# Attention and scan kernel on one core: empty places that do preparation work, an end of its own for the last block, and program order on every engine

## The chip, the cores and the metric

The kernel runs on one core of one Trainium2 chip. A core has five engines that run at the same time and meet through semaphores: TensorE (PE in the profile; its weight loads are PEld), VectorE (DVE), ScalarE (ACT), GpSimd (POOL) and SyncE (SP), which issues the transfers here. The metric is the device time of one execution in microseconds. Before the change it is 3108.49 us, the median of three runs (3106.8 to 3109.73).

## The reference

Four images of 128 channels by 4096 positions go through two layers, all in float32. Cut to what matters:

```python
# layer 0, per image: x is (128, 4096) after a group norm
v, gate = split(sigmoid(conv_bn(x, Wvg)))
q, k    = conv_bn(x, Wq) * SCALE, conv_bn(x, Wk)        # 64 channels each
out     = softmax(q.T @ k) @ v.T * gate                 # 4096 x 4096 scores
x       = x0 + conv_bn(out, Wp)

# layer 1, per image: t is (4096, 128), h = layernorm(t)
q       = h @ W
t       = t + softmax(q @ q.T) @ h                      # symmetric scores
Wx      = layernorm(t) @ Wffn.T
# over all four images:
Wx      = batchnorm(Wx)                                 # mean and variance over 16384 rows
y_t     = sigmoid(Wx_t + y_(t-1) @ V.T)                 # a scan over 4096 steps
x       = t + y
```

## The kernel before

For each image the kernel runs `layer0` and `layer1`; the scan follows behind all four. It works in blocks of 512 queries (`NB` = 8 per image). In `layer0` a block is 16 pairs of key tiles. In `layer1` the scores are symmetric: a block of scores `(n, a)` with `a < n` is used once as it stands (`direct`) and once transposed (`reversed_products`), so its exponentials `e` are transposed by VectorE into `dd`, turned further by 16 transfers into `tt`, and multiplied four steps later.

What is left to do for a finished block, and what prepares the next image, is cut into small functions. They wait in two queues, `pending` and `ahead`, and the main loops take one function from a queue in each step, so that its instructions come between the large products:

```python
        ahead: deque = deque()
        pending: deque = deque()

        def nothing():
            pass
        ...
        def flush(until=None):
            while pending and until not in done:
                pending.popleft()()

        def attention(score_mm, bias, scale, weigh, finish, need):
            ...
            for n in range(NB):
                acc = first = None
                for p in range(PAIRS):
                    need(n, p)
                    ps = ps_s.tile([P, 2, QB], F32, tag="s", name="ps")
                    for h in range(2):                              # scores of a pair
                        lhsT, rhs = score_mm(n, p, h)
                        nc.tensor.matmul(ps[:, h, :], lhsT=lhsT, rhs=rhs, start=True, stop=True)
                    e = ep.tile([P, 2, QB], F32, tag="e", name="e")
                    nc.scalar.activation(e, ps, AF.Exp, scale=scale)
                    ...                                             # acc += e on VectorE
                    fifo.append((n, p, e, acc))
                    if len(fifo) > LAG:                             # LAG = 2
                        pop()                                       # value products of pair p - 2
                        ...
                    if ahead:
                        ahead.popleft()()
                    elif pending and (p % 2 == 0 or len(pending) > 6):
                        pending.popleft()()
```

`layer0` puts `[sums, nothing, denominators, projection, nothing, tokens]` in `pending` for each finished block; `nothing` leaves time for a transfer. `sums` and `projection` each end in `move`, which turns a tile through memory: one transfer out and four in.

The layer norm over the 128 channels of each row, used by both layers:

```python
        def layernorm(src, dst):
            ...
            for j in range(NQ):                       # NQ = 4
                nc.vector.bn_stats(s6, src[j])
                nc.vector.bn_aggr(mv[:, j, :], s6)
            inv_sqrt(rstd, mv[:, :, 1], EPS_LN)       # two instructions on GpSimd
            for j in range(NQ):
                nc.vector.tensor_scalar(dst[j], src[j], mv[:, j, 0:1], rstd[:, j : j + 1],
                                        ALU.subtract, ALU.mult)
```

The preparation of an image: `stats`, `mean`, `variance`, `normalise`, then `queries_keys` and `values` for chunks of 512 positions, then `gate`. For image 0 the first chunk is done ahead of everything, and `need` makes sure that the rest is ready in time; for the others the functions go into `ahead` and are taken during `layer1` of the image before.

```python
            def queries_keys(ch):
                m = bank(False)
                nc.tensor.matmul(m, lhsT=wt["qk"], rhs=xg[:, cs], start=True, stop=True)
                nc.vector.tensor_scalar(q[lo, cs], m[lo, :], ...)
                nc.scalar.activation(q[hi, cs], m[lo, :], AF.Identity, ...)
                nc.vector.tensor_scalar(k[...], m[hi, :], ...)

            def values(ch):
                m = bank(True)
                for i in range(4):
                    nc.tensor.matmul(m[:, bass.ts(i, P)], lhsT=xg[...], rhs=wt["vs"], ...)
                nc.vector.tensor_tensor(vc, m, bc, ALU.add)
                nc.scalar.activation(vc, vc, AF.Tanh, scale=0.5)
                nc.vector.tensor_scalar(vc, vc, 0.5, 0.5, ALU.mult, ALU.add)
        ...
        def need(n, p):
            if n == 0:
                while p // 4 > 0 and n_ahead - len(ahead) < 6 * (p // 4):
                    ahead.popleft()()
```

A step of `layer1`, and what a finished block leaves to do there:

```python
                    for i in range(2):
                        ...                                        # 2 score products, 2 exponentials,
                        ...                                        # 2 transposes into dd if turned
                        fifo.append((n, a, i, e, o))
                        clock += 1
                        if len(fifo) > LAG:
                            direct()
                        if turned and turned[0][0] <= clock:
                            reversed_products()                    # 4 products with tt, VectorE sums
                        if pending:
                            pending.popleft()()
                        elif ahead:
                            ahead.popleft()()
                    if turns(n, a):
                        ...                                        # 16 transfers tt <- dd
                        turned.append((clock + 4, n, a, t))

            def finish(n):
                ...
                nc.sync.dma_start(t, t_d[b, n])
                def tokens():     # mt: 4 transposes of oacc; t1 = mt * rinv + t; h2 = layernorm(t1)
                def result():     # mr: 4 transposes of t1; ScalarE copies; store to t2_d
                def turn():       # mh: 4 transposes of h2; ScalarE copies to th
                def inputs():     # mw: product of wt["f"] and th; bn_stats; copy to wx or wxs
                if b == B - 1 and n == 0:
                    pending.extend([tokens, turn, inputs, result])
                else:
                    pending.extend([tokens, result, turn, inputs])
```

All four take their PSUM bank from `ps_m`, which has one buffer; `h2`, `th`, `t1` and `t2` have one buffer each in the pool `work`.

Behind the last block come a range test over all denominators (`ok`), the pools of the scan, and the scan:

```python
        ok = big.tile([P, 2, 2 * B * NT], F32, tag="oacc", name="ok")
        ...                                                        # two compares, one reduction
    with ExitStack() as st:
        scan = st.enter_context(tc.tile_pool(name="scan", bufs=1))
        ...
        mv = scan.tile([P, 2], F32, name="bn_mv")
        nc.vector.bn_aggr(mv, bn_st.rearrange("p a b -> p (a b)"))
        gain = scan.tile([P, 1], F32, name="gain")
        inv_sqrt(gain, mv[:, 1:2], EPS_BN)
        ...
        for k, i in enumerate(steps):                              # 44 steps of 2 halves
            ...                                                    # product with V, sigmoid on ScalarE,
                                                                   # VectorE: preload, t2 += y
```

The order in which an engine's instructions stand in the built program is not the order in which the code emits them: a scheduler chooses it at compile time, by priority and by its own estimate of times.

Of the kernel before, what the change touches and what calls it, by code (L numbers as in the profile page):

```python
# [18 lines left out]
P = 128  # L19
B, C, N = 4, 128, 4096  # L20
DQ = 64
# [28 lines left out]
def conv_attn_hybrid_kernel(  # L50
# [78 lines left out]
    def inv_sqrt(dst, var, eps):  # L129
# [5 lines left out]
    fast(  # L135
        tc, x, out, t_d, t2_d, wxs_d, turn_d,
        dict(qk=w[:, DQ : DQ + P], vs=w_vs, g=w_g, ps=w_ps, a=w_a, f=w_f, vt=v_t),
        col, par, par2, bpc, bc, ident, gavg, quart, own, shift, inv_sqrt, par_ok,
    )
# [18 lines left out]
def fast(  # L158
# [7 lines left out]
    den_all = keep.tile([P, 2 * B * NT], F32, name="den_all")  # L166

    with ExitStack() as st:
# [14 lines left out]
        def nothing():  # L183
            pass
# [8 lines left out]
        def attention(score_mm, bias, scale, weigh, finish, need):  # L193
# [3 lines left out]
            o = None  # L197

# [9 lines left out]
# [5 lines that stand above are left out]
                    for h in range(2):  # L213
# [4 lines that stand above are left out]
                    if p == 0:  # L218
                        first = e
                    elif p == 1:  # L220
                        acc = accp.tile([P, 2, QB], F32, tag="acc", name="acc", bufs=2)
                        nc.vector.tensor_tensor(acc, first, e, ALU.add)
                    else:
                        nc.vector.tensor_tensor(acc, acc, e, ALU.add)  # L224
                    fifo.append((n, p, e, acc))
                    if len(fifo) > LAG:
                        pop()
                        if p == 0:
                            pop()
                    if ahead:  # L230
                        ahead.popleft()()
                    elif pending and (p % 2 == 0 or len(pending) > 6):
                        pending.popleft()()
# [232 lines left out]
        def layer1(b, h, qt):  # L466
# [74 lines left out]
            def finish(n):  # L541
# [3 lines left out]
                h2 = work.tile([P, NQ, C], F32, tag="h2", name="h2")  # L545
                th = work.tile([P, QB], F32, tag="th", name="th")
                t1 = work.tile([P, NQ, C], F32, tag="og", name="t1b")
                nc.sync.dma_start(t, t_d[b, n])

                def tokens():  # L550
# [4 lines left out]
                    m = ps_m.tile([P, NQ, P], F32, tag="m", name="mt")  # L555
# [10 lines left out]
                def result():  # L566
                    m = ps_m.tile([P, QB], F32, tag="m", name="mr")
                    for j in range(NQ):
                        nc.tensor.transpose(m[:, bass.ts(j, P)], t1[:, j, :], ident)
                    t2 = work.tile([P, QB], F32, tag="xb", name="t2")  # L570
                    nc.scalar.copy(t2, m)
                    nc.sync.dma_start(t2_d[b, :, cs], t2)

                def turn():
                    m = ps_m.tile([P, QB], F32, tag="m", name="mh")
# [4 lines left out]
                def inputs():  # L580
                    m = ps_m.tile([P, QB], F32, tag="m", name="mw")
# [10 lines left out]
                if b == B - 1 and n == 0:  # L592
                    pending.extend([tokens, turn, inputs, result])
                else:
                    pending.extend([tokens, result, turn, inputs])
# [106 lines left out]

        ok = big.tile([P, 2, 2 * B * NT], F32, tag="oacc", name="ok")
# [5 lines left out]
    with ExitStack() as st:  # L709
# [19 lines left out]
        mv = scan.tile([P, 2], F32, name="bn_mv")  # L729
        nc.vector.bn_aggr(mv, bn_st.rearrange("p a b -> p (a b)"))  # L730
        gain = scan.tile([P, 1], F32, name="gain")
# [3 lines left out]
        bias = scan.tile([P, 1], F32, name="bias")  # L735
# [458 lines left out]
```

## Time and profile before

| | |
|---|---|
| time, median of 3 | 3108.49 us |
| span of the profiled run | 3106.2 us |
| granted TensorE clock | 0.993 |
| first TensorE product | 16.25 us |
| first product of the scan | 3020.77 us |
| last store issued, end | 3082.6 us, 3106.2 us |

A line of the group lists reads: line of the code, engine, operation, tile written and tiles read, sizes, count; then busy time and mean length of one; then how long the engine stood idle just before these instructions, and what ended that idle time. A line of the list of waits reads: who waited, for whom, us in total, times, longest. A line of the timeline reads: start, length, engine, line, operation, tiles, count, and in brackets the idle time before it with what ended it. A line of the list by stretch reads: from, to, length, then busy time and count for each engine (PE, PEld, DVE, ACT, POOL), the granted clock, and the transfers' share and rate. One product in the code with 512 columns is two records here; a record on all 128 rows has 0.429 us to the next, one on half of the rows (L215, L394, two halves side by side) 0.214 us on average.

### The profile page before, as it was taken

To read this page: it belongs to the slowest core of one execution; us is meant where nothing else is said; L and a number is where in the kernel's file an instruction comes from. 1 tells how busy PE (TensorE), PEld (TensorE's weight loads), DVE (VectorE), ACT (ScalarE), POOL (GpSimd) and SP (SyncE) were. 2 spreads that over 40 slices of the span, in tenths; PEclk is the share of its full clock that TensorE was granted. 3 is DMA by queue.
4 is the path that set the end of the run, shared out by engine and by line. 5 is a ranking of instruction groups with operands and counts; after the bars stand their busy time and mean duration, and the time that the engine had idled before them with its cause. 6 is when DMAs were issued, how large, how long until landed. Compare 5 with 4: busy or idle time off the path is not lost.

```text
span 3106.2 us, 32252 instructions
## 1 busy us (share of the span) xinstructions
PE 3018.6 (97%) x10706; PEld 1362.3 (44%) x10706; DVE 1877.7 (60%) x3160; ACT 1144.8 (37%) x2018; POOL 144.5 (5%) x183
## 2 busy tenths in 40 slices
PE   7999999999999999999999999999999999999976
PEld 3444444444444444444444444444444444444432
DVE  6666656555666665655566666555566666455546
ACT  3444433333344443333334443333334444323324
POOL 0000000000000000000000000000000000000000
PEclk9999999999999999999999999999999999999988
DMA  1011143333111123334211114333321113443423
GB/s 51 28 55 55 55 111 88 91 89 92 46 55 55 55 78 93 90 89 97 73 52 55 50 43 116 88 91 93 91 56 55 49 44 121 114 104 88 98 98 157
DMA packets 233168, 241.14 MB, mean 78 GB/s; under 512 B 88480, under 2 KB 144288, under 8 KB 231968
## 3 DMA queue, kind: packets, MB, share of 16 engines
q1 hardware_dynamic: 231984, 238.18, 28.2%
q8 instruction: 88, 1.44, 0.2%
q10 hardware_dynamic: 1008, 0.79, 0.1%
q14 instruction: 88, 0.72, 0.1%
HBM read 65.80 MB, written 56.62 MB: 39 GB/s over the span
## 4 chain that ended last, share of the span: by engine, by line
PE 91%; DVE 4%; SPq 1%; POOL 1%; DMA 1%; issue 1%; ACT 0%; ACTq 0%; DVEq 0%; POOLq 0%
PE o L394 28%; PE ps L215 15%; PE ps L613 15%; PE o L501 14%; PE ot L514 12%; SPq L650 1%; PE m L243 1%; PE mw L582 1%; PE mq L487 1%; PE mp L326 1%; PE ps_r L764 1%; PE mh L577 1%; POOL rstd L132 1%; DVE t1b L559 1%; PE mp L361 1%; PE mp L346 1%
## 5 line engine op out<-in xcount | busy, mean ns | idle before, releaser
L394 PE MATMUL o<-e,nxt 64*128 64x512 f32 x4096 | 963.8, 589 | 0.0
L217 ACT ACTIVATE e<-ps 128x1024 f32<-128x1024 f32 x512 | 521.4, 1025 | 674.7 <-PE ps L215 657.5
L224 DVE TENSOR_TENSOR acc<-acc,e 128x1024 f32<-128x1024 f32 x448 | 547.6, 1222 | 236.4 <-ACT e L217 220.5
L619 ACT ACTIVATE e<-ps,shift 128x512 f32<-128x512 f32 x580 | 393.9, 684 | 749.8 <-PE ps L613 497.1
L394 PEld LDWEIGHTS o<-e,nxt 64*128 64x128 f32 x4096 | 399.0, 187 | 482.3 <-issue 474.5
L613 PE MATMUL ps<-qt 128*128 128x512 f32 x1160 | 547.8, 595 | 2.7 <-ACT qt L488 2.7
L501 PE MATMUL o<-e,h 128*128 128x512 f32 x1160 | 537.7, 592 | 0.0
L215 PE MATMUL ps<-nxt 64*128 64x512 f32 x2048 | 534.5, 596 | 1.2 <-DVE nxt L338 0.9
L514 PE MATMUL ot<-tt,h 128*128 128x512 f32 x888 | 399.8, 593 | 0.0
L624 DVE STREAM_TRANSPOSE dd<-e 128x512 f32<-128x512 f32 x444 | 286.5, 686 | 83.4 <-ACT e L619 73.1
L501 PEld LDWEIGHTS o<-e,h 128*128 128x128 f32 x1160 | 218.3, 191 | 260.7 <-issue 259.5
L613 PEld LDWEIGHTS ps<-qt 128*128 128x128 f32 x1160 | 213.4, 191 | 249.0 <-issue 224.2
L215 PEld LDWEIGHTS ps<-nxt 64*128 64x128 f32 x2048 | 194.5, 187 | 231.5 <-issue 158.8
L514 PEld LDWEIGHTS ot<-tt,h 128*128 128x128 f32 x888 | 167.9, 190 | 210.0 <-issue 205.7
L519 DVE TENSOR_REDUCE slots<-tt 128x4 f32<-128x2048 f32 x111 | 250.7, 2258 | 9.7 <-DMA tt<-dd 9.4
L528 DVE TENSOR_TENSOR oacc<-oacc,ot 128x512 f32<-128x512 f32 x87 | 59.3, 682 | 209.8 <-PE ot L514 209.8
L131 POOL TENSOR_SCALAR rstd<-mv 128x4 f32<-128x4 f32 x64 | 14.6, 228 | 2456.5 <-DVE mv L268 2456.5
L619 ACT ACTIVATION_READ_ACCUMULATOR e<-ps,shift 128x1 f32 x580 | 113.9, 196 | 0.0
L448 DVE SCALAR_TENSOR_TENSOR t<-yt,rinv,t 128x128 f32<-128x128 f32 x128 | 36.6, 347 | 71.5 <-DMA yt<-turn_d 71.4
L411 POOL TENSOR_SCALAR xb<-xb,bpc 128x512 f32<-128x512 f32 x32 | 57.4, 1793 | 318.0 <-DMA xb<-in_x_dram 289.3
L132 POOL TENSOR_TENSOR rstd<-rstd,mhalf 128x4 f32<-128x4 f32 x64 | 66.4, 1038 | 5.3
L271 DVE TENSOR_SCALAR h<-t,mv,rstd 128x128 f32<-128x128 f32 x128 | 35.7, 343 | 47.1 <-POOL rstd L132 47.1
(134 smaller groups left out, 1491.7 us busy)
## 6 DMA issues: line engine op xcount, KB each, us to landing
tt<-dd SPq DMA_DIRECT2D x1776, 64.0 KB, 2.0
turn_d<-d SPq DMA_DIRECT2D x96, 256.0 KB, 2.0
t_d<-t SPq DMA_DIRECT2D x64, 256.0 KB, 2.0
nxt<-in_x_dram SPq DMA_DIRECT2D x16, 512.0 KB, 5.5
xb<-in_x_dram SPq DMA_DIRECT2D x32, 256.0 KB, 2.9
t<-turn_d SPq DMA_DIRECT2D x128, 64.0 KB, 2.0
yt<-turn_d SPq DMA_DIRECT2D x128, 64.0 KB, 2.0
qt<-turn_d SPq DMA_DIRECT2D x128, 64.0 KB, 2.0
```

Source lines behind the costliest of these rows:

```text
L132: nc.gpsimd.tensor_tensor(dst, dst, mhalf[:, :n], ALU.pow)
L215: nc.tensor.matmul(ps[:, h, :], lhsT=lhsT, rhs=rhs, start=True, stop=True)
L217: nc.scalar.activation(e, ps, AF.Exp, scale=scale)
L224: nc.vector.tensor_tensor(acc, acc, e, ALU.add)
L394: nc.tensor.matmul(o[r], lhsT=v[rs, p + h * PAIRS, :], rhs=e[rs, h, :], start=(p == 0 and h == 0), stop=(p == PAIRS - 1 and h == 1),)
L501: nc.tensor.matmul(o, lhsT=h[:, NQ * a + 2 * i + half, :], rhs=e[:, half, :], start=(a == order(n)[0] and i == 0 and half == 0), stop=(a = ...
L514: nc.tensor.matmul(ot, lhsT=h[:, NQ * n + j, :], rhs=t[:, :, j, :, :].rearrange("q p k j -> q k p j"), start=(j == 0), stop=(j == NQ - 1),)
L519: nc.vector.tensor_reduce(slots[:, bass.ts(n, NQ), a], t.rearrange("q p b k j -> q b p (k j)"), AX.XY, ALU.add,)
L528: nc.vector.tensor_tensor(oacc[:, n, :], oacc[:, n, :], o, ALU.add)
L613: nc.tensor.matmul(ps[:, half, :], lhsT=qt[:, bass.ts(at, P)], rhs=qt[:, bass.ts(n, QB)], start=True, stop=True,)
L619: nc.scalar.activation(e[:, half, :], ps[:, half, :], AF.Exp, bias=shift, accum_out=slots[:, at, n : n + 1],)
L624: nc.vector.transpose(d.rearrange("q f b k j -> q k b f j")[:, 2 * i + half], e[:, half, :].rearrange("q (b f j) -> q b f j", b=NQ, f=NQ),)
```

## The change

It has four parts:

- *Empty places.* `nothing` now takes a function from `ahead`, if there is one, and two such places stand between `result` and `turn` in `layer1`. In `attention`, functions that were in `pending` at the start are taken in every step.
- *An end of its own.* The last block of the last image puts `tokens` at the head of the queue, brings `result` ahead of `turn`, takes its tiles from the pool of `e` and its PSUM banks from the scores' pool.
- *Ahead of the scan.* The BatchNorm's small tiles lie in the pool `keep` instead of the scan's own, and one sigmoid on a single column is issued before the range test, so that the table of that function is loaded there.
- *Program order.* The whole of `fast` stands under `tc.manual_schedule()`: each engine, SyncE included, gets its instructions in the order in which the code emits them.

It is meant to keep TensorE from waiting for the layer norm, to shorten the chain between the last attention product and the scan, and to make the order of work that of the loop.

```diff
--- before.py
+++ after.py
@@ -132,11 +132,12 @@
         nc.gpsimd.tensor_tensor(dst, dst, mhalf[:, :n], ALU.pow)
 
     par_ok = const.tile([P, 4], F32, name="par_ok")
-    fast(
-        tc, x, out, t_d, t2_d, wxs_d, turn_d,
-        dict(qk=w[:, DQ : DQ + P], vs=w_vs, g=w_g, ps=w_ps, a=w_a, f=w_f, vt=v_t),
-        col, par, par2, bpc, bc, ident, gavg, quart, own, shift, inv_sqrt, par_ok,
-    )
+    with tc.manual_schedule():
+        fast(
+            tc, x, out, t_d, t2_d, wxs_d, turn_d,
+            dict(qk=w[:, DQ : DQ + P], vs=w_vs, g=w_g, ps=w_ps, a=w_a, f=w_f, vt=v_t),
+            col, par, par2, bpc, bc, ident, gavg, quart, own, shift, inv_sqrt, par_ok,
+        )
 
 
 
@@ -164,6 +165,10 @@
     keep = keep_ctx.enter_context(tc.tile_pool(name="keep", bufs=1))
     bn_st = keep.tile([P, B * NB, 6], F32, name="bn_st")
     den_all = keep.tile([P, 2 * B * NT], F32, name="den_all")
+    mv = keep.tile([P, 2], F32, name="bn_mv")
+    gain = keep.tile([P, 1], F32, name="gain")
+    bias = keep.tile([P, 1], F32, name="bias")
+    first_y = keep.tile([P, 1], F32, name="first_y")
 
     with ExitStack() as st:
         big = st.enter_context(tc.tile_pool(name="big", bufs=1))
@@ -181,7 +186,10 @@
         pending: deque = deque()
 
         def nothing():
-            pass
+
+
+            if ahead:
+                ahead.popleft()()
 
         done = set()
 
@@ -195,6 +203,7 @@
 
             fifo: deque = deque()
             o = None
+            left = len(pending)
 
             def pop():
                 nonlocal o
@@ -229,7 +238,8 @@
                             pop()
                     if ahead:
                         ahead.popleft()()
-                    elif pending and (p % 2 == 0 or len(pending) > 6):
+                    elif pending and (p % 2 == 0 or left > 0 or len(pending) > 6):
+                        left -= 1
                         pending.popleft()()
             while fifo:
                 pop()
@@ -542,9 +552,22 @@
                 cs = bass.ts(n, QB)
                 rinv = stat.tile([P, NQ], F32, tag="rinv", name="rinv")
                 t = work.tile([P, 4, NQ, 32], F32, tag="t", name="t1", bufs=2)
-                h2 = work.tile([P, NQ, C], F32, tag="h2", name="h2")
-                th = work.tile([P, QB], F32, tag="th", name="th")
-                t1 = work.tile([P, NQ, C], F32, tag="og", name="t1b")
+                if b == B - 1 and n == 0:
+
+                    one, two = (ep.tile([P, 2, QB], F32, tag="e", name="last") for _ in range(2))
+                    h2, t1 = (one[:, r, :].rearrange("q (j c) -> q j c", j=NQ) for r in range(2))
+                    th, t2 = two[:, 0, :], two[:, 1, :]
+
+                    def bank():
+                        return ps_s.tile([P, 2, QB], F32, tag="s", name="ml")[:, 0, :]
+                else:
+                    h2 = work.tile([P, NQ, C], F32, tag="h2", name="h2")
+                    th = work.tile([P, QB], F32, tag="th", name="th")
+                    t1 = work.tile([P, NQ, C], F32, tag="og", name="t1b")
+                    t2 = None
+
+                    def bank():
+                        return ps_m.tile([P, QB], F32, tag="m", name="m1")
                 nc.sync.dma_start(t, t_d[b, n])
 
                 def tokens():
@@ -552,7 +575,7 @@
                     den = den_all[:, at : at + NQ]
                     nc.vector.tensor_reduce(den, slots[:, bass.ts(n, NQ), :], AX.X, ALU.add)
                     nc.vector.reciprocal(rinv, den)
-                    m = ps_m.tile([P, NQ, P], F32, tag="m", name="mt")
+                    m = bank().rearrange("q (j c) -> q j c", j=NQ)
                     for j in range(NQ):
                         nc.tensor.transpose(m[:, j, :], oacc[:, n, bass.ts(j, P)], ident)
                     for j in range(NQ):
@@ -564,21 +587,23 @@
                     layernorm(quarters(t1), quarters(h2))
 
                 def result():
-                    m = ps_m.tile([P, QB], F32, tag="m", name="mr")
+                    nonlocal t2
+                    m = bank()
                     for j in range(NQ):
                         nc.tensor.transpose(m[:, bass.ts(j, P)], t1[:, j, :], ident)
-                    t2 = work.tile([P, QB], F32, tag="xb", name="t2")
+                    if t2 is None:
+                        t2 = work.tile([P, QB], F32, tag="xb", name="t2")
                     nc.scalar.copy(t2, m)
                     nc.sync.dma_start(t2_d[b, :, cs], t2)
 
                 def turn():
-                    m = ps_m.tile([P, QB], F32, tag="m", name="mh")
+                    m = bank()
                     for j in range(NQ):
                         nc.tensor.transpose(m[:, bass.ts(j, P)], h2[:, j, :], ident)
                     nc.scalar.copy(th, m)
 
                 def inputs():
-                    m = ps_m.tile([P, QB], F32, tag="m", name="mw")
+                    m = bank()
                     nc.tensor.matmul(m, lhsT=wt["f"], rhs=th, start=True, stop=True)
                     nc.vector.bn_stats(bn_st[:, b * NB + n, :], m)
                     m = m.rearrange("p (g i s) -> p i g s", i=L // 2, s=2)
@@ -590,9 +615,12 @@
                         nc.sync.dma_start(wxs_d[b, :, :, bass.ts(n, GB), :], wx)
 
                 if b == B - 1 and n == 0:
-                    pending.extend([tokens, turn, inputs, result])
+                    pending.appendleft(tokens)
+                    pending.extend([result, turn, inputs])
+                elif b == B - 1 and n < 4:
+                    pending.extend([tokens, result, turn, inputs])
                 else:
-                    pending.extend([tokens, result, turn, inputs])
+                    pending.extend([tokens, result, nothing, nothing, turn, inputs])
 
 
             for n in [NB - 2, NB - 1] + list(range(NB - 3, -1, -1)):
@@ -700,6 +728,8 @@
                 ahead.popleft()()
         flush()
 
+
+        nc.scalar.activation(first_y, shift, AF.Sigmoid)
         ok = big.tile([P, 2, 2 * B * NT], F32, tag="oacc", name="ok")
         nc.vector.tensor_scalar(ok[:, 0, :], den_all, DEN_LO, None, ALU.is_ge)
         nc.vector.tensor_scalar(ok[:, 1, :], den_all, DEN_HI, None, ALU.is_le)
@@ -726,13 +756,10 @@
                     banks[s][i][:, : HB * G], lhsT=ident, rhs=wxs[:, 0, :HB, :, 0],
                     start=True, stop=True, skip_group_check=True,
                 )
-        mv = scan.tile([P, 2], F32, name="bn_mv")
         nc.vector.bn_aggr(mv, bn_st.rearrange("p a b -> p (a b)"))
-        gain = scan.tile([P, 1], F32, name="gain")
         inv_sqrt(gain, mv[:, 1:2], EPS_BN)
         nc.vector.tensor_mul(gain, gain, col(GAMMA))
 
-        bias = scan.tile([P, 1], F32, name="bias")
         nc.vector.tensor_mul(bias, mv[:, 0:1], gain)
         nc.vector.tensor_sub(bias, col(BETA), bias)
```

## The prediction, written before the result was known

> **What bounds the kernel now.** I read the page's busy line and chain first, then busy time by stretch, then TensorE's waits, then the timeline of the places where TensorE stands still.
>
> ```profile
> PE 3018.6 (97%) x10706; PEld 1362.3 (44%) x10706; DVE 1877.7 (60%) x3160; ACT 1144.8 (37%) x2018; POOL 144.5 (5%) x183
> ...
> PE 91%; DVE 4%; SPq 1%; POOL 1%; DMA 1%; issue 1%; ACT 0%; ACTq 0%; DVEq 0%; POOLq 0%
> ```
>
> TensorE carries 91% of the chain that ended last; nothing else comes near. The change adds and removes no matrix product, so only TensorE's standing time, and the stretches in which TensorE is not the limit, can move. Busy time by stretch (start, warm-up, the eight attention stages, their end, the scan, the last store) says how much that is:
>
> ```profile
> 0.00:16.25 16.25, 0.00 (x0) 0.03 (x1) 7.28 (x17) 1.28 (x1) 3.68 (x13) 1.00 0.61 194
> ...
> 100.00:2950.00 2850.00, 2829.21 (x10062) 1273.80 (x10059) 1727.71 (x2852) 1047.07 (x1846) 131.97 (x156) 1.00 0.29 76
> 2950.00:3020.77 70.77, 53.95 (x155) 25.67 (x153) 33.12 (x100) 17.58 (x43) 5.98 (x11) 0.90 0.19 61
> 3020.77:3081.30 60.53, 55.19 (x172) 27.10 (x172) 53.60 (x113) 42.12 (x87) 0.00 (x0) 0.97 0.30 129
> ```
>
> The second column of numbers is TensorE's busy time. In 2850 us of attention it stands only 20.8 us; in the 71 us of their end 16.8 us; before its first product 16.25 us. The scan runs on VectorE (53.6 of 60.5), and nothing in the change touches its work. TensorE's waits name the standing time:
>
> ```profile
> PE mh L577 <- DVE h L271: 15.7, 21, 4.4
> PE ps_r L764 <- ACT y L761: 7.8, 1, 7.8
> ...
> PE mp L346 <- DVE nxt L351: 2.4, 3, 0.8
> PE mp L326 <- DVE nxt L351: 2.4, 3, 0.8
> ```
>
> The first is the one that repeats: `turn` transposes the layer norm's result `h2` and stands until VectorE has written it. Why it is not written is seen in one such place:
>
> ```profile
> 585.60 1.12 DVE L559 SCALAR_TENSOR_TENSOR t1b<-mt,rinv,t 128x128 f32<-128x128 f32 x4
> ...
> 588.77 1.04 POOL L132 TENSOR_TENSOR rstd<-rstd,mhalf 128x4 f32<-128x4 f32 x1
> 589.84 1.11 DVE L271 TENSOR_SCALAR h<-t1b,mv,rstd 128x128 f32<-128x128 f32 x4 [1.47 <-POOL rstd L132]
> ...
> 590.33 0.49 PE L577 MATMUL mh<-ident,h 128*128 128x128 f32 x2 [0.65 <-DVE h L271]
> ```
>
> The norm takes 5.4 us from 585.60 to 590.95, and the scheduler has put the transposes 4.7 us behind its start. (The products `mt` that feed it ran at 567.98, nearly 18 us sooner.) The end shows a chain of single steps:
>
> ```profile
> 3006.50 1.15 PE L577 MATMUL mh<-ident,h 128*128 128x128 f32 x4 [4.39 <-DVE h L271]
> ...
> 3015.81 1.02 DVE L730 BATCH_NORM_AGGREGATE bn_mv<-bn_st 128x2 f32<-128x192 f32 x1 [4.03 <-DMA t_d<-t]
> ...
> 3018.81 1.28 ACT L761 ACT_TABLE_LOAD   x1 [5.24 <-DVE bias L737]
> ...
> 3020.77 1.65 PE L764 MATMUL ps_r<-y,w 128*128 128x256 f32 x3 [7.82 <-ACT y L761]
> ```
>
> The BatchNorm aggregate waits for a store of the last result, since its tile lies in memory that the store still reads; then the sigmoid's table is loaded between `bias` and the first `y`.
>
> **What the Trainium skill says.** *PSUM — Partial Sum Buffer*, section "Engine vs sequencer instructions": the queues of ScalarE, VectorE and GpSimd are strict FIFO, and matmuls start and complete in program order. So an early instruction that is not ready holds all behind it, and order is all that this change alters in the middle; the trace agrees (VectorE idles 1.47 us at L271 while other work is pending). *Perfetto Trace Analysis*, "Identifying the Most-Contended Engine": matmul busy time is no good measure of how near TensorE is to its limit. Agreed: L577 shows 0.65 us idle above where the starts of the products lie 0.81 us further apart than their 0.11 or 0.43 us of pace; I therefore count by starts. *ScalarE: Activation LUTs*, "What ACT_TABLE_LOAD costs": about 1283 ns; the trace has 1.28 us. *DMA: Bandwidth & Descriptors*, "Anatomy of one DMA": a fixed 2 us or so, for GpSimd's path; the page here has 2.0 us for SyncE's `turn_d` and `tt`.
>
> **The change part by part.**
>
> *Empty places.* In blocks of layer 1 `turn` now comes four places after `tokens`. A place is one step of the loop, at least four score and four value matmuls of 0.429 us, 3.4 us. In the order of the built program `mh` thus stands over 10 us behind `mt`, the norm needs about 5.4 us plus 1.2 for its inputs, and the wait goes. By starts: 14.2 us of the 18.6 us shown idle at L577 belong to the middle; times 0.81/0.65 that is 17 us. The four transposes also run at the pace at which VectorE writes `h2` (27.9 us busy against 20.0 for the equal `mr`); I count 4 us. An empty place now pops preparation work of the next image, so no place is lost.
>
> *Program order, what it mends.* The scheduler had put two `values` matmul groups back to back on the single bank `ps_m`; six stalls, 0.78 us shown, 0.95 by starts, 5.7 us. In program order a step has one item, and they go. At the start VectorE normalised six chunks (3.48 us at 19.30) and transposed `xb` (0.71 at 15.14) before work that TensorE waits for; in program order it normalises two and goes on: 1.4 + 1.2 = 2.6 us.
>
> *Own end.* The last block's `tokens` is first in the queue and has its own banks, the store is sooner, `mv` and `bias` lie outside the scan's memory, the table is loaded early. From the last value matmul (2994.9) to the first `y` (3020.7) are 25.8 us now. After: the norm of block 1 before it on VectorE (a wait of 2.6), `mt` 0.5, `t1b` to `h2` 5.4, `mh`, copy and `mw` 2.7, two statistics and a copy 1.3, the range test, now in line, 1.1, aggregate 1.0, POOL 0.9, three small ops 0.5, `y` 0.7: 16.7. Saved 9 us.
>
> *Program order, what it costs.* (a) In warm-up `need` pops two `values` in a row ahead of scores 4, 8 and 12, with one spare bank. VectorE must first finish q (0.80), wait for ScalarE's copy (0.77), k (0.82) and the sum (0.69), so the second group waits about 3 us, three times: 9 us. (b) At the start of layer 1 the first 16 `tt` transfers (10 us of issuing on SyncE) now stand behind both moves of the last block instead of between them; before they landed 2.8 us ahead of their product. I count 1.7 us by four images: 7 us. (c) `gm` follows its aggregate directly: 1.2 by 3, 4 us. (d) `tokens` of block 6 follows its last sum directly (0.95 us by 4), 4 us. (e) `t1b` follows `mt` at once, and its load is late by SyncE's backlog (issued 4 us after `mt` in the place above, 3.0 us to landing); result comes 3.4 us later, so mostly covered: 3 us.
>
> Sum: 17 + 4 + 5.7 + 2.6 + 9 = 38 saved; 9 + 7 + 4 + 4 + 3 = 27 lost. 3108 - 38 + 27 = 3097; I say 3096.
>
> **The rivals.** *The order costs nothing:* the loop was written with a lag of two and its slack hides (a) to (e); then 3070 to 3078. For it speaks that layer 0 already runs without gaps. *An early wait blocks VectorE:* (e) is larger, because `t1b` waiting for a transfer also holds the `dd` transposes, so `tt` come late and `ot` stands, some 4 us by 28 blocks, over 100 us: 3200. For it speaks that the scheduler had kept `t1b` 14 to 18 us behind `mt`, against it that transfers land 7 to 14 us ahead of `ot` in most places, and SyncE's issuing (10.0 to 10.7 us for 16) keeps up with a turn of 24 matmuls at 0.429, 10.3 us, plus small items. *Only the end counts:* the middle's waits move to other places and 3099 remains.
>
> **Range and chances.** All gains together cannot exceed the standing time by starts, about 104 us (from the first product to the scan are 3004.5 us, and the groups hold 6272 half products at 0.214, 3464 full ones at 0.429 and 640 small ones at 0.11, 2901 us), less the fixed switches between half and full tiles; for 2%, 62 us would have to go, and I find 38 before costs. So faster by over 2% has 0.02. The first rival sets the low end, 3074; an early wait in part sets the high end, 3124; its full form is the 0.04 of slower. The rest, 0.94, is within 2%.
>
> **What would show it.** Right: L577's wait for `h` gone outside the end; no `nxt` waits at L346 in layer 1; from last value matmul to first `y` about 17 us, no wait for `t_d` at the aggregate; warm-up to 100 us with new TensorE waits at L346 for VectorE. Wrong: TensorE waits at `ot` for `tt` or VectorE, or at `mr` for `t1b`, of more than 10 us in sum, or a layer 0 that no longer runs without gaps.

## The result and the profile after

The changed kernel takes 3152.6 us (median of 4, 3151.9 to 3156.15) against 3107.64 us of the kernel before beside it. The ratio is 1.0146, 95% interval 1.0128 to 1.0164: 45 us slower, where 12 us faster was predicted, and above the predicted range.

The page after, its busy line and its chain:

```profile
PE 3022.7 (96%) x10706; PEld 1373.9 (44%) x10706; DVE 1920.2 (61%) x3160; ACT 1145.4 (36%) x2019; POOL 137.2 (4%) x183
...
PE 88%; DVE 4%; SPq 3%; DMA 2%; ACT 1%; issue 1%; POOL 0%; DVEq 0%; ACTq 0%; POOLq 0%
```

TensorE has the same 10706 products, but its share of the chain falls from 91% to 88%; the queue of SyncE (SPq) rises from 1% to 3% and transfers (DMA) from 1% to 2%. TensorE's waits, longest first (who waits, for whom, us in total, times, longest):

```profile
PE gm L313 <- DVE gmv L311: 36.6, 4, 14.9
PE ot L524 <- DMA tt<-dd: 20.2, 5, 11.0
PE ps L224 <- ACT e L226: 11.9, 5, 2.5
PE po L356 <- DVE nxt L361: 7.5, 3, 2.5
PE n_ok L148 <- DVE par_ok L818: 5.5, 1, 5.5
PE m L580 <- DVE oacc L538: 3.1, 4, 0.8
```

The wait that led before, the transposes `mh` for `h`, is gone from the middle. In its place stand three that no image paid before: the group average `gm` of the next image (14.9 us of its 36.6 are the start of the kernel, as before), the turned products `ot` waiting for their transfers, and scores of layer 0 waiting for an exponential.

To see where the 44 us between the two profiled runs (3106.2 and 3150.2) lie, I took the time from each product's start to the next one's, less its pace (0.429 us for a full product, 0.2145 for a half one, 0.109 for a 128-column transpose, 0.216, 0.028 and 0.010 for 256, 1 and 16 columns), and summed this standing time by stretch. With the start and the tail it adds up to the span less 2942.6 us in both kernels, so nothing is lost between the rows:

| standing time of TensorE, us | before | after | difference | the prediction's terms for it |
|---|---|---|---|---|
| before the first product | 16.3 | 14.9 | -1.4 | -2.6 |
| first product to 100 us | 16.8 | 24.5 | +7.7 | +9 (a) |
| layer 0 | 21.6 | 39.7 | +18.1 | 0 |
| first 80 us of layer 1, four images | 5.1 | 65.2 | +60.1 | +7 (b), +4 (c) |
| rest of layer 1 | 36.1 | 5.6 | -30.5 | -17 - 4 - 5.7, +4 (d), +3 (e) |
| last value product to first `y` | 19.5 | 11.3 | -8.2 | -9 |
| scan, last store | 48.2 | 46.4 | -1.8 | 0 |
| sum | 163.5 | 207.5 | +44.0 | -11 |

Two rows hold the error; the rest of layer 1 came out 11 us better than its terms (-30.5 against -19.7). The first of the two is the start of layer 1. The timeline of image 0 there (start, length, engine, line, operation; SPq rows are SyncE issuing transfers):

```profile
418.62 1.99 PE L641 MATMUL ps<-qt 128*128 128x512 f32 x4
...
420.82 0.34 SPq L265 DMA_DIRECT2D turn_d<-d  x1
...
423.65 1.73 SPq L267 DMA_DIRECT2D yt<-turn_d  x4
...
425.42 10.34 SPq L678 DMA_DIRECT2D tt<-dd  x16
...
436.48 0.40 SPq L265 DMA_DIRECT2D turn_d<-d  x1
437.27 5.40 PE L524 MATMUL ot<-tt,h 128*128 128x512 f32 x8 [2.94 <-DMA tt<-dd]
...
439.91 1.74 SPq L267 DMA_DIRECT2D qt<-turn_d  x4
...
441.70 20.79 SPq L678 DMA_DIRECT2D tt<-dd  x33
...
453.37 1.30 DVE L652 STREAM_TRANSPOSE dd<-e 128x512 f32<-128x512 f32 x2 [8.42 <-DMA tt<-dd]
454.60 0.33 DVE L311 BATCH_NORM_AGGREGATE gmv<-gs 128x2 f32<-128x48 f32 x1
455.07 0.56 PE L313 MATMUL gm<-gmv,gavg 128*128 128x1 f32 x2 [8.11 <-DVE gmv L311]
455.49 3.65 PE L641 MATMUL ps<-qt 128*128 128x512 f32 x4
```

Read it from below. TensorE stands 8.1 us at `gm`, because its aggregate comes 0.47 us ahead of it. The aggregate is late because VectorE stood 8.4 us ahead of it, at a transpose into `dd`. `dd` has two buffers, and this one was still being read by the second batch of `tt`, which SyncE began to issue only at 441.70. It was ready to be turned at about 427 (the transposes into it end at 427.18). Ahead of it in SyncE's line stood the first batch (10.3 us), a move out (436.48), its landing, and the four transfers in (439.91). From the end of a move's issue to its transfers in, SyncE itself stands 2.5 us (421.16 to 423.65) and 3.0 us (436.88 to 439.91), and all behind it stands too.

The scheduler had done this otherwise in the kernel before; SyncE's rows of the same place:

```profile
409.86 1.37 SPq L255 DMA_DIRECT2D turn_d<-d  x1
...
411.28 1.78 SPq L650 DMA_DIRECT2D tt<-dd  x3
413.16 1.97 SPq L257 DMA_DIRECT2D yt<-turn_d  x4
...
415.17 4.94 SPq L650 DMA_DIRECT2D tt<-dd  x8
```

While a move lands, three `tt` transfers are issued.

The second row is layer 0, once per image. The same line of SyncE, where block 1 of image 1 has just been finished:

```profile
900.50 0.34 SPq L265 DMA_DIRECT2D turn_d<-d  x1
...
902.53 1.74 SPq L267 DMA_DIRECT2D qt<-turn_d  x4
...
904.38 0.38 SPq L420 DMA_DIRECT2D xb<-in_x_dram  x1
...
907.29 1.57 POOL L421 TENSOR_SCALAR xb<-xb,bpc 128x512 f32<-128x512 f32 x1 [8.71 <-DMA xb<-in_x_dram]
908.90 0.71 DVE L262 STREAM_TRANSPOSE d<-xb 128x512 f32<-128x512 f32 x1 [3.92 <-POOL xb L421]
...
910.81 1.02 ACT L226 ACTIVATE e<-ps 128x1024 f32<-128x1024 f32 x1 [4.69 <-DVE acc L231]
...
911.89 1.15 PE L224 MATMUL ps<-nxt 64*128 64x512 f32 x4 [2.42 <-ACT e L226]
```

The load of `xb` stands behind the move of `tokens`. It lands late, GpSimd adds late, VectorE waits 3.92 us at the transpose of `xb`, and the sums `acc` behind it hold the buffers of `e` back, so ScalarE and then TensorE stand.

### The profile page after: what moved, and what is told of

It is laid out like the page before. It is cut to its first block, busy times and chain, and to the rows that moved or that the text cites. A ratio compares the mean times of both kernels' runs of the same rounds, so it can differ in the third digit from the quotient of the medians.

```text
span 3150.2 us, 32358 instructions
## 1 busy us (share of the span) xinstructions
PE 3022.7 (96%) x10706; PEld 1373.9 (44%) x10706; DVE 1920.2 (61%) x3160; ACT 1145.4 (36%) x2019; POOL 137.2 (4%) x183
## 4 chain that ended last, share of the span: by engine, by line
PE 88%; DVE 4%; SPq 3%; DMA 2%; ACT 1%; issue 1%; POOL 0%; DVEq 0%; ACTq 0%; POOLq 0%
PE o L404 26%; PE ps L641 15%; PE o L511 14%; PE ps L224 14%; PE ot L524 12%; SPq L678 2%; DMA turn_d<-d 1%; PE m L253 1%; PE m L607 1%; PE mp L336 1%; PE mp L356 1%; SPq L267 1%; PE mp L371 1%; DVE ps_r L778 1%; DVE t2s L805 1%
## 5 line engine op out<-in xcount | busy, mean ns | idle before, releaser
L652 DVE STREAM_TRANSPOSE dd<-e 128x512 f32<-128x512 f32 x444 | 299.0, 703 | 301.7 <-ACT e L647 225.2
L524 PE MATMUL ot<-tt,h 128*128 128x512 f32 x888 | 406.4, 601 | 20.2 <-DMA tt<-dd 20.2
L414 DVE TENSOR_TENSOR og<-o,og 128x512 f32<-128x512 f32 x32 | 22.1, 690 | 117.7 <-ACT og L413 117.7
L132 POOL TENSOR_TENSOR rstd<-rstd,mhalf 128x4 f32<-128x4 f32 x64 | 66.4, 1037 | 5.3
L538 DVE TENSOR_TENSOR oacc<-oacc,o 128x512 f32<-128x512 f32 x24 | 16.5, 687 | 79.6 <-PE o L511 79.6
```

What stands on the lines that cost most here:

```text
L132: nc.gpsimd.tensor_tensor(dst, dst, mhalf[:, :n], ALU.pow)
L524: nc.tensor.matmul(ot, lhsT=h[:, NQ * n + j, :], rhs=t[:, :, j, :, :].rearrange("q p k j -> q k p j"), start=(j == 0), stop=(j == NQ - 1),)
L538: nc.vector.tensor_tensor(oacc[:, n, :], oacc[:, n, :], o, ALU.add)
L652: nc.vector.transpose(d.rearrange("q f b k j -> q k b f j")[:, 2 * i + half], e[:, half, :].rearrange("q (b f j) -> q b f j", b=NQ, f=NQ),)
```

## The experiments

Theory A: SyncE's program order makes the loss, since a transfer that waits for another's landing holds every transfer behind it. Theory B: the program order of the compute engines makes it, above all VectorE's and TensorE's. Each ratio is to the kernel before.

**e1: SyncE in the scheduler's order, the other four in program order.**

```diff
-    with tc.manual_schedule():
+    with tc.manual_schedule(engines={E.PE, E.DVE, E.Activation, E.Pool}):
```

> The changed kernel, with program order on TensorE, VectorE, ScalarE and GpSimd, and SyncE's transfers left to the scheduler. Theory A (the loss of 45 us comes from SyncE's program order: transfers that must wait, the moves through memory, stand ahead of the tt transfers at the start of each layer 1 and ahead of the xb load in layer 0, and VectorE and TensorE are held behind them): the 57 us lost at the four starts of layer 1 fall to 15 or less and the 17 us in layer 0 go, 3085 to 3100 us. Theory B (program order on VectorE and TensorE is itself the loss, since products follow their producer directly): 3135 us or more.

Measured: 3121.7 us (3118.8 to 3128.5), ratio 1.0048 (1.0034 to 1.0062). This is between the two, so neither theory holds alone. The standing time of layer 0 returns to 23.8 us; the start of layer 1 keeps 48.0:

```profile
PE gm L314 <- DVE gmv L312: 37.5, 4, 15.1
PE ot L525 <- DMA tt<-dd: 7.6, 1, 7.6
```

TensorE's waits at `ot` fall from 20.2 to 7.6 us, those at `gm` stay. The run does not take the late transfers away: VectorE's waits for them at `dd` fall only from 74.3 to 53.9 us, and the second batch of image 0, its `dd` ready at 424.7, is issued at 435.51, behind another move.

**e2: no program order anywhere.** The rest of the change stays: the empty places, the end of its own and what was moved ahead of the scan.

```diff
-    with tc.manual_schedule():
+    with ExitStack():
```

> The changed kernel without program order on any engine: the empty places and the own end alone, as the scheduler orders them. Both theories: the end gains some 9 to 11 us, the waits of mh shrink in part, 3085 to 3102 us. It tells what the other parts of the change bring, and so how much program order loses (50 to 65 us).

Measured: 3074.4 us (3074.1 to 3074.9), ratio 0.9892 (0.9876 to 0.9909). This beats the kernels before and after by 33 and 78 us, and lies below the 3085 to 3102 us expected. The start of layer 1 stands 5.2 us, the rest of it 7.7. So the other parts of the change bring about what was hoped of them (33 us), and program order costs 78 us on top, more than the 50 to 65 expected. The timeline of the same place shows what the scheduler does with `gm`:

```profile
406.96 0.37 DVE L311 BATCH_NORM_AGGREGATE gmv<-gs 128x2 f32<-128x48 f32 x1
...
432.90 0.28 PE L313 MATMUL gm<-gmv,gavg 128*128 128x1 f32 x2
```

The statistics and the aggregate are done early on VectorE, 26 us ahead of the product.

**e3: program order on SyncE alone.**

```diff
-    with tc.manual_schedule():
+    with tc.manual_schedule(engines={E.SP}):
```

> The changed kernel with program order on SyncE alone; the four compute engines are left to the scheduler. Theory A: most of the loss is there, 3125 to 3150 us. Theory B: no loss, the time of the version without any program order, 3085 to 3102 us.

Measured: 3143.4 us (3138.6 to 3145.5), ratio 1.0109 (1.0092 to 1.0126), as A expected. SyncE's line alone costs 3143.4 - 3074.4 = 69 us, the four others alone 3121.7 - 3074.4 = 47, all five 78. The costs overlap. With SyncE alone the loss sits elsewhere (layer 0 stands 58.3 us, the rest of layer 1 32.5, its start only 16.0), presumably because the scheduler arranges the other engines by estimates that do not know of the fixed line; that is argued, not shown.

**e4: the load of `xb` on ScalarE's queue**, all else as changed.

```diff
-                nc.sync.dma_start(xb, x[b, :, cs])
+                nc.scalar.dma_start(xb, x[b, :, cs])
```

> The changed kernel, but the load of xb in layer 0 is issued by ScalarE instead of SyncE, so that it no longer stands behind the move of the block before. Theory A: the four waits of scores for exponentials in layer 0 (2.4 us each, and the half clock behind them, 17 us in all) go, 3133 to 3138 us, and the starts of layer 1 stay as they are. Theory B (VectorE would be late there anyway): 3150 to 3155 us.

Measured: 3139.0 us (3136.2 to 3141.4), ratio 1.0097 (1.0080 to 1.0114). That is 1 us above A's figure. Layer 0 falls from 39.7 to 23.9 us of standing time, the start of layer 1 stays (66.4). So the chain read in the second timeline is the cause of layer 0's share: 15.8 us of its standing time, 13.6 of the kernel's.

**e5: `gm` two places behind its aggregate**, all else as changed. No function is added: the last four `bn_stats` share a place with `bn_aggr`.

```diff
-            norm = [partial(stats, i) for i in range(4)] + [mean, variance]
+            norm = [partial(stats, i) for i in range(2)] + [rows, rest, mean, variance]
```

> The changed kernel (3152.6) with one difference: in the preparation of an image the product gm no longer stands directly behind its aggregate in TensorE's line; the last four bn_stats and bn_aggr make one place, the next place is empty, then comes gm. Theory A (SyncE's program order: the transfers are late, whatever stands behind them waits): the wait at gm goes, but since the transposes into dd still wait for the late transfers, TensorE waits at ot instead, and the time stays at 3140 to 3152. Theory B (the order of the compute engines: TensorE stands at gm only because gm has no slack behind an aggregate that VectorE reaches late): the three waits of 7 to 8 us at gm and the slow products behind them go and nothing takes their place, 3118 to 3130.

Measured: 3140.2 us (3137.8 to 3140.9), ratio 1.0105 (1.0088 to 1.0121): at the lower edge of A's figure, far above B's. The waits beyond the start at `gm` are gone, and others grow:

```profile
PE ot L531 <- DMA tt<-dd: 24.5, 8, 11.4
PE gm L320 <- DVE gmv L313: 15.0, 1, 15.0
...
PE mq L504 <- DVE nxt L355: 7.3, 3, 2.6
```

TensorE waits more often at `ot` (8 times, not 5). While the transfers are late, giving one product slack moves most of the wait.

**e6: the moves on GpSimd's queue.** Program order stays on every engine, but a move's landing holds up GpSimd and no `tt`.

```diff
         def move(blocks, dst):
...
-            nc.sync.dma_start(via, d)
+            nc.gpsimd.dma_start(via, d)
             for a in range(4):
-                nc.sync.dma_start(dst[...], ...)
+                nc.gpsimd.dma_start(dst[...], ...)
```

> The changed kernel with the five transfers of every move issued by GpSimd instead of SyncE; the order on every engine stays the program's. No tt transfer and no load of xb then stands behind a transfer that waits for another's landing. Theory A: the waits of layer 0 (17 us) go, the waits at ot in layer 1 fall below 9 us, and of the waits at gm only what VectorE's order makes stays: 3105 to 3125. Theory B: the starts of layer 1 stay as they are, 3140 to 3152.

Measured: 3112.7 us (median of 20, 3107.3 to 3120.5), ratio 1.0017 (1.0010 to 1.0024), within A's 3105 to 3125. One edit that leaves the order alone takes back 40 of the 45 us. The timeline:

```profile
417.21 10.50 SPq L678 DMA_DIRECT2D tt<-dd  x16
420.12 0.56 POOL L265 DMA_DIRECT2D turn_d<-d  x1 [3.95 <-DVE d L262]
...
431.56 30.92 SPq L678 DMA_DIRECT2D tt<-dd  x48
...
445.53 0.33 DVE L311 BATCH_NORM_AGGREGATE gmv<-gs 128x2 f32<-128x48 f32 x1
446.00 0.56 PE L313 MATMUL gm<-gmv,gavg 128*128 128x1 f32 x2 [4.91 <-DVE gmv L311]
```

The first `tt` is issued at 417.21 instead of 425.42, the second batch at 431.56 instead of 441.70; the wait at `gm` shrinks to 4.9 us. The moves themselves are no quicker there: from issue to landing one transfer out takes a median 2.4 us from GpSimd and 2.0 from SyncE. What changed is what stands behind them, and at this place the landing waits hurt little on GpSimd. In layer 0 they hurt, against A's expectation: it stands 30.3 us (23.9 in e4), since GpSimd's addition to `xb`, loaded by an issue at 887.11, now stands behind the move of `tokens`:

```profile
894.59 2.19 POOL L267 DMA_DIRECT2D qt<-turn_d  x4 [2.05 <-DMA turn_d<-d]
896.82 1.58 POOL L421 TENSOR_SCALAR xb<-xb,bpc 128x512 f32<-128x512 f32 x1
...
898.44 0.71 DVE L262 STREAM_TRANSPOSE d<-xb 128x512 f32<-128x512 f32 x1 [2.34 <-POOL xb L421]
```

**e7: both edits, moves on GpSimd and `gm` two places later.**

> Both edits of the two kernels beside it: moves issued by GpSimd, and gm two places behind its aggregate. If the loss consists of SyncE's blocking plus gm's missing slack, this takes back both: 3082 to 3098, and TensorE's waits beyond the start are those of the warm-up (9 us) and of tokens of block 6 (4 us). If the loss has another cause in the order of the compute engines, it stays above 3105.

Measured: 3095.4 us (3094.1 to 3096.7), ratio 0.9961 (0.9946 to 0.9975), as expected. Beside the waits named there, 5.4 us at the scores of layer 0, 3.5 at `ot` and 3.2 at `mq` remain. The start of layer 1 stands 15.3 us. Once the transfers are in time, `gm`'s slack is worth 17 us; without that (e5) it was worth 12.

**e8: the end alone.** The scheduler's order, no function in the empty places, no added places.

```diff
         def nothing():
-            if ahead:
-                ahead.popleft()()
+            pass
...
-                    pending.extend([tokens, result, nothing, nothing, turn, inputs])
+                    pending.extend([tokens, result, turn, inputs])
```

> The scheduler's order on every engine, no function in the empty places and no extra places: of the change only the end of its own, the BatchNorm tiles in the other pool and the early table load. By the sum of the prediction the end is worth 9 us: 3096 to 3101. If the end is worth more and the places little, it comes near the 3074 of the kernel that also has the places: 3074 to 3085.

Measured: 3102.1 us (median of 15, 3099.7 to 3106.6), ratio 0.9984 (0.9976 to 0.9992), 1 us above the 3096 to 3101 expected of the end alone. The end is worth 5.0 us by the medians and 8.0 by the standing time between last value product and `y` (19.5 to 11.5). The other 3102.1 - 3074.4 = 28 us of e2 are the places: the rest of layer 1 stands 37.8 us here and 7.7 there.

**e9: as e7, and in the warm-up one more function ahead of each odd step**, so that no two `values` follow each other directly.

```diff
             if n == 0:
+                if p < 12 and p % 2 == 1:
+                    ahead.popleft()()
                 while p // 4 > 0 and n_ahead - len(ahead) < 6 * (p // 4):
```

> The kernel with the moves on GpSimd and gm two places behind its aggregate (3095.4), and in the warm-up the functions taken at need are spread: one more ahead of every odd step, so that two values groups never follow each other directly. By term (a) of the prediction (three stalls of 3 us, 9 us): 3085 to 3089, and the waits of TensorE at po for nxt go. If VectorE is simply short of time in the warm-up, the waits move to the exponentials or to q and k and the time stays at 3093 to 3097.

Measured: 3088.2 us (3087.4 to 3090.3), ratio 0.9941 (0.9924 to 0.9958). It takes back 7.2 us; the three waits of 2.5 us at `po` are gone, and the warm-up's standing time falls from 25.9 to 18.4 us. This is the best version in program order found here.

**e10 and e11: which compute engine's line?** e10 has program order on VectorE alone, e11 on TensorE, ScalarE and GpSimd.

```diff
-    with tc.manual_schedule():
+    with tc.manual_schedule(engines={E.DVE})                        # e10
+    with tc.manual_schedule(engines={E.PE, E.Activation, E.Pool})   # e11
```

> The changed kernel with the program's order on VectorE alone; TensorE, ScalarE, GpSimd and SyncE in the scheduler's order. If the loss of 47 us that the four compute engines' order makes (3121.7 against 3074.4) comes from VectorE's line, in which the aggregate ahead of gm stands behind the transposes into dd that wait for transfers, it stays above 3105. If it comes from TensorE's line (gm directly behind its aggregate), 3072 to 3085.

> The counterpart: the program's order on TensorE, ScalarE and GpSimd, the scheduler's on VectorE and SyncE. If VectorE's line is the cause: 3072 to 3090, and gm has no wait beyond the start. If TensorE's line is: above 3105. If it takes both, each alone is near 3074 to 3090 and neither is the cause by itself.

Measured: e10 3085.7 us (3084.2 to 3087.0), ratio 0.9932 (0.9916 to 0.9949); e11 3088.6 us (3087.9 to 3091.4), ratio 0.9943 (0.9926 to 0.9959). Neither has a wait at `gm` beyond the start. Each half costs little over e2 (11 and 14 us), and together they cost 47. It takes both: with VectorE free the aggregate goes ahead (e11: aggregate at 404.08, `gm` at 430.18), with TensorE free `gm` is put later (e10: 441.69 and 447.60).

All runs side by side:

| kernel | us | to 100 us | layer 0 | layer 1, first 80 us | layer 1, rest |
|---|---|---|---|---|---|
| before | 3107.6 | 16.8 | 21.6 | 5.1 | 36.1 |
| after | 3152.6 | 24.5 | 39.7 | 65.2 | 5.6 |
| e1 SyncE free | 3121.7 | 25.9 | 23.8 | 48.0 | 5.6 |
| e2 no order | 3074.4 | 19.0 | 23.4 | 5.2 | 7.7 |
| e3 SyncE only | 3143.4 | 19.5 | 58.3 | 16.0 | 32.5 |
| e4 `xb` elsewhere | 3139.0 | 25.5 | 23.9 | 66.4 | 5.5 |
| e5 `gm` later | 3140.2 | 24.5 | 38.6 | 50.3 | 5.5 |
| e6 moves elsewhere | 3112.7 | 25.9 | 30.3 | 33.6 | 5.5 |
| e7 both | 3095.4 | 25.9 | 30.2 | 15.3 | 5.6 |
| e8 end only | 3102.1 | 17.6 | 21.6 | 5.1 | 37.8 |
| e9 and warm-up | 3088.2 | 18.4 | 29.1 | 15.8 | 5.7 |
| e10 VectorE only | 3085.7 | 21.2 | 23.1 | 12.7 | 9.3 |
| e11 without VectorE | 3088.6 | 17.5 | 23.0 | 24.1 | 5.4 |

Between e9 and e2 remain 14 us, 6 in layer 0 and 11 at the starts of layer 1, less what e9 gains elsewhere. I did not take them apart. One candidate for layer 0 is the addition to `xb` shown at e6: in e9 VectorE still waits for it 9.3 us in all, four times up to 2.3 us. One for the starts, not tried, is left on SyncE: the `tt` batches of the first pass come faster than they are issued (48 transfers in 30.9 us without a pause in e6).

## Why the prediction was wrong

The saved side was right in kind and too small: 38 us were predicted, and the table of stretches has 30.5 + 8.2 + 1.4 + 1.8 = 42, although 30.5 is net of (d) and (e). The lost side failed: 27 us were predicted, and 7.7 + 18.1 + 60.1 = 86 came.

- *Empty places, right; the order's gain, half.* The waits at `mh` for `h` are gone outside the end. The prediction gave 21 us to the places and 5.7 to program order, for the two `values` groups on one bank. e2 has no program order and stands 7.7 us in the rest of layer 1, so the places alone do both. In program order three of the six stalls stay: `mq` now follows `queries_keys` on the one bank of `ps_m` and waits for `nxt` three times 0.8 us (1.0 by starts); e2 has no such wait. (In the first term, 14.2 times 0.81/0.65 is 17.7 us, not 17.)
- *Own end, right.* 9 us predicted, 8.2 measured, 16.7 us against 17.6 from the end of the last value product to the first `y`. The steps came as listed: the table load lies ahead of the test (1.28 us at 3059.76), and no store holds the aggregate.
- *Start.* 2.6 us predicted, 1.4 measured ahead of the first product.
- *(a) Warm-up, right.* Three waits of 2.5 us (2.67 by starts), where 3 us were predicted. The 7.7 us of the stretch and the 7.2 of e9 answer to the 9.
- *(d) right, (e) nil at TensorE.* Four waits of 0.8 us (0.94 by starts) at `m` for `oacc`. `t1b` waits for its load 5.7 us on VectorE in all, and TensorE does not notice.
- *(b) and (c), the failed steps.* "Now stand behind both moves of the last block instead of between them; before they landed 2.8 us ahead of their product. I count 1.7 us by four images: 7 us." The prediction took the ten us of issuing and left out that SyncE stands still between a move out and the move in (420.82 to 423.65, 436.48 to 439.91 above). With that the first batch is issued at 425.42 and the second starts 14.5 us after its `dd` is ready. And the estimate ended at `ot`. The lateness goes on: with two buffers of `dd`, late `tt` stop VectorE's transposes (74.3 us of waiting for `tt` transfers after, 9.7 before). Behind these stands the aggregate, and behind the aggregate, with no slack, TensorE. "`gm` follows its aggregate directly: 1.2 by 3, 4 us" took the aggregate as in time. The first 80 us of layer 1 lost 60.1 us, not 11; some 14 of them are lost by the products behind the stands, at half clock (last section), for which the prediction had no term at all. e6 and e7 cut this row to 33.6 and 15.3 us with edits that touch only the moves' place in the queues and `gm`'s place.
- *Layer 0 "already runs without gaps", wrong as an argument for the order.* It ran so in the order of the scheduler. In program order the load of `xb` stands behind a move: 18.1 us (e4 takes back 13.6).

Of the rivals, *an early wait blocks VectorE* had the right form (VectorE held by a transfer, `tt` late, `ot` waits) and the wrong place: not `t1b` in 28 blocks, but `dd` at the four starts, where moves and batches meet. What the prediction named as proof against itself, waits at `ot` over 10 us and gaps in layer 0, both came.

## What to carry to other kernels

Before fixing an issue order by hand, list for each queue that also issues transfers which of them waits for another's landing, and ask what independent work stands behind it: at the places above SyncE stood 1.7 to 3.0 us for each such pair, and the engines behind it added theirs. A product written directly behind the VectorE result that it reads has no slack once the order is fixed on both engines; give it a place or two, and follow a late transfer through the buffers that it holds rather than only to its own reader. Try the parts of a change apart: here the two useful ones together were worth 33 us and were hidden under an order that cost 78.

## What the hardware showed beside this

Products behind a longer stand ran at half their pace. After the 8.1 us at `gm` the four scores at 455.49 took 3.65 us where four such take 1.88 to 1.99 in the same timeline. By stretch (from, to, length, busy times and counts, then the granted clock):

```profile
909.40:912.00 2.60, 0.18 (x4) 0.11 (x3) 2.50 (x3) 1.02 (x1) 0.00 (x0) 1.00 0.27 104
912.00:917.00 5.00, 5.00 (x16) 2.14 (x18) 4.39 (x9) 1.02 (x1) 0.00 (x0) 0.66 0.22 52
917.00:930.00 13.00, 13.00 (x63) 5.81 (x61) 6.64 (x7) 5.70 (x6) 0.00 (x0) 1.00 0.13 42
455.00:458.00 3.00, 2.93 (x5) 1.60 (x6) 0.54 (x3) 0.00 (x0) 0.00 (x0) 0.50 0.42 104
```

The clock is granted at half for some microseconds and then again in full (0.66 is the mean of a stretch of 5.00 us, 3.41 of them at half). Between 90 and 2950 us the changed kernel has twelve stands of over 2 us. They last 54 us by starts, and the products of the 6 us behind each lose 20 us more in sum, of which 0.1 to 0.7 each is what such stretches lose anyway. The two come to 74 of the 78 us by which layer 0 and the starts of layer 1 grew. The prediction had no such term, and could not read it from the middle of the kernel before, which had no stand over 1.1 us and no half clock.

The Trainium skill has this: *TensorE: Matmul & The Clock Gate*, section "HAM oscillation — how this bites in real kernels", warns of idle gaps of more than about 3.4 us, behind which the array runs at half its clock. The runs agree on the half, and on long gaps: between 100 and 2950 us, in the nine traces here that have any, each gap of 3.3 us or more is followed by 1.5 to 3.4 us lost. They differ on the limit: gaps between 2.0 and 3.2 us lost anything from 0.1 to 3.3 us at like lengths, often 1.8 (the one above is 2.67 us by starts), and in e8 two gaps of 0.95 us, the second 1.9 us behind the first, were followed by 3.41 us at half clock, 1.8 us lost.

The traces show why like gaps cost unlike amounts. In each of the 13, every change of the granted clock lies a whole number of periods of 3.413 us from the others, and between 100 and 2950 us the clock falls to half 42 times, for one to four periods (3.41 to 13.65 us). Each time TensorE had stood at least 2.07 us in sum within the one period that ended there; of the 10741 full-clock periods with no fall behind them, 31 had stood as long. So it is mostly the sum within a period that decides, and a gap shared between two periods can go free: one of 2.72 us in e3 (at 1995.0) had 2.13 us in the fuller one and was followed by a loss of 0.1 us.
